# A two-layer attention and graph kernel: the first stretch with ScalarE and VectorE in a written order, and rows' low parts ahead of masks

## The chip, the cores and the metric

The kernel runs on one core of a Trainium2 chip. A core has several engines, each with its own stream of instructions: TensorE (PE in the profile) multiplies matrices and writes only to PSUM, the accumulator memory; VectorE (DVE) and ScalarE (ACT) do elementwise work and read PSUM out; GpSimd (POOL) does small work here and issues loads of weights; SyncE (SP) issues the other transfers between DRAM and SBUF, the core's working memory. ScalarE issues a few transfers too. The metric is the device time of one execution in microseconds (us).

## The reference

x has 64 graphs of 256 nodes with 512 features; adj is one 256 x 256 matrix of zeros and ones that all graphs share. Layer 0 is attention with 8 heads of 64, layer 1 is a product with adj; each adds its input and is normalised.

```python
q, k, v = x @ Wq + bq, x @ Wk + bk, x @ Wv + bv          # heads of 64
scores = einsum('bqhd,bkhd->bhqk', q, k) / sqrt(64)
scores = scores + (1 - adj) * -1e9
out = einsum('bhqk,bkhd->bqhd', softmax(scores), v).reshape(b, n, d)
x = layernorm(x + out @ Wo + bo)
y = einsum('nm,bmd->bnd', adj, x)
x = layernorm(x + y @ W1 + b1)
```

## The kernel before

Work goes by pairs of graphs, p = 0 to 31 (`NP` = 32). All products with weights are made from three parts: a value is split into a high part, a low part and a difference (`high`, `low`, `diff`), and a block of output is 3 x 4 matmuls of 128 x 512 (`product`, L298). A pair takes 4 blocks each with wv ("v"), wq and wk ("q", "k"), wo ("o") and w1 ("l"). Splitting takes ScalarE for the high part (`x_high`, `set_high`) and VectorE for the other two (`rest`, L252). For weights ScalarE works a second time, on the low part (`split`, L121).

**Weights.** Each of five sets of split weights (v, qk1, qk0, o, l) is 3 MB. They are split once, stored in DRAM (`keep`, L129, issued on SP), and loaded again for each pair by `load_w` (issued on POOL) into `wring`, six buffers of 1 MB, three for a set. The stages follow in the order of `STAGES` (L100). wv, wq and wk are split straight in the ring (`split_in_ring`), wo and w1 beside it (`split_aside`, L152), into three of the four buffers named `sh`; wo is read from the `sl` buffers, w1 from `sd`. The same names hold split operands later (`set_high`).

**Attention.** `scores` multiplies k and q and lets ScalarE take the exponential; `masked` multiplies by adj on VectorE and `summed` adds over key chunks (`masks` is two of the first and one of the second); `values` sums the weights for the softmax and multiplies with v. Its `between` list is issued between ScalarE's copy of the sums (`zc`) and of the values (`vc`).

**Layer 1.** The normalised rows are split in two (`hl_high` on ScalarE, `hl_low` on VectorE) into tiles named `hl`, one for each graph b and half of the features. `adj_x(p, b, half)` multiplies such a tile with adj and splits the result out of PSUM (`set_high` on ScalarE, `rest` on VectorE). `hl` comes from the pool `two`, and PSUM tiles of all blocks and of `adj_x` from `ps_mm`:

```python
two = pool("two", 2)
ps_at = pool("ps_at", 5, space=bass.MemoryType.PSUM)
ps_mm = pool("ps_mm", 3, space=bass.MemoryType.PSUM)
```

**Order.** The functions `start`, `first`, `second` and `last` list tasks for `do`, which issues them one by one. Inside `tc.manual_schedule(engines=...)` the named engines execute in the order of the program; instructions of other engines, and of SP's and POOL's queues, are ordered by the framework's planner. `start` and `last` fix TensorE alone; the loop over w = 1 to 31 fixes TensorE, VectorE and ScalarE. In pass w, `first(w)` finishes the attention of pair w − 1 and does blocks v, q and k of pair w and blocks o of w − 1; `second(w)`, w = 1 to 30, does scores of w, the early q and k blocks of w + 1, and layer 1 of w − 1. A tile of a pool whose buffers are all taken waits until the last reader of an earlier tile is done, on whichever engine that reader is; the instruction that first writes the tile does this waiting.

In `start`, the first pair's x is transposed by TensorE in four groups (`x_first`), each copied out of PSUM by ScalarE and VectorE; later pairs are loaded in 64 KB pieces (`load_x`) and transposed by VectorE (`x_t`). `load_r` loads the rows for the residual into tiles named `r`, which at first hold the raw wq and wk.

Of the kernel before, what the change touches and what calls it, by code (L numbers as in the profile page):

```python
# [8 lines left out]
F32 = mybir.dt.float32  # L9
F32R = mybir.dt.float32r  # L10
I32 = mybir.dt.int32
AF = mybir.ActivationFunctionType
# [3 lines left out]
P = 128  # L16
# [19 lines left out]
def fast(tc, x, adj, wq, bq, wk, bk, wv, bv, wo, bo, w1, b1, out):  # L36
# [34 lines left out]
    RAW, SCRATCH, W = {}, {}, {}  # L71
# [10 lines left out]
    def load_r(p):  # L82
        if p < NP:
            t = two.tile([P, 2, NC, D], F32, name="r")
            nc.sync.dma_start(t, xr[p])
            R[p] = [t[:, b] for b in range(2)]
# [34 lines left out]
    def split(raw, parts):  # L121

        high, low, diff = parts
        nc.scalar.activation(high, raw, AF.Copy, scale=CUT)
        nc.vector.scalar_tensor_tensor(low, high.bitcast(F32), -RHO, raw, op0=OP.mult, op1=OP.add)
        nc.vector.scalar_tensor_tensor(diff, high.bitcast(F32), -1 / FINE, low.bitcast(F32), op0=OP.mult, op1=OP.add)
        nc.scalar.activation(low, low.bitcast(F32), AF.Copy, scale=FINE / RHO)
# [8 lines left out]
    def split_in_ring(stage, k):  # L136

        name, p = stage
        if k == 0:
            W[stage] = ring(name)  # L140
        t = [w[:, k // 2, k % 2] for w in W[stage]]
        if name == "v":
            split(RAW["v", k], t)
        else:
            g, which = int(name[2]), "qk"[k // 2]
            raw = RAW[which][:, 2 * (k % 2):2 * (k % 2) + 2, g * HF:(g + 1) * HF]
            split(raw, [u.rearrange("p (k e) -> p k e", k=2) for u in t])
        if k == DC - 1:
            for i in range(3):
                keep(name, i, None, W[stage][i])  # L150

    def split_aside(name, k):  # L152
        t = [four.tile([P, D], F32R, name="sh") for _ in range(3)]
        split(RAW[name, k], t)
        for i in range(3):
            keep(name, i, k, t[i])
# [33 lines left out]
    for k in range(DC):  # L190
        RAW["l", k] = four.tile([P, D], F32, name="sd")
        nc.sync.dma_start(RAW["l", k], w1[k * P:(k + 1) * P])
# [7 lines left out]
    def adj_t():  # L200
# [4 lines left out]
        nc.vector.tensor_copy(adjT, pt)  # L205

# [184 lines left out]
    def masks(p, g, b):  # L391
        return [(masked, p, g, b, 0), (masked, p, g, b, 1), (summed, p, g, b)]
# [74 lines left out]
    def do(*tasks):  # L467
        for t in tasks:
            for f, *args in (t if isinstance(t, list) else [t]):
                f(*args)  # L470
# [9 lines left out]
    def first(w):  # L480
# [4 lines left out]
        do((inverse, q - 1, "l", 1), masks(w, 0, 0),  # L485
# [4 lines left out]
           (block, "v", w, 2), (x_t, n, 0), (block, "v", w, 3), (x_t, n, 1), (stage_end, w),  # L490
           (block, "q", w, 2), (block, "k", w, 2), (block, "q", w, 3), (block, "k", w, 3), (stage_end, w),
# [7 lines left out]
    def second(w):  # L499
# [5 lines left out]
           (adj_x, q, 0, 0), masks(w, 1, 0),  # L505
           (block, "k", n, 0), (hl_high, q, 1, 0), (hl_high, q, 1, 1), (hl_low, q, 1, 0), (hl_low, q, 1, 1),
# [7 lines left out]

    def start():
        do(*((x_first, i) for i in range(4)))
        do((block, "q", 0, 0), (split_in_ring, ("v", 0), 0), (block, "k", 0, 0), (split_in_ring, ("v", 0), 1),
           (x_high, 0, 0), (x_high, 0, 1), (x_rest, 0, 0), (x_rest, 0, 1),
           (block, "q", 0, 1), (split_in_ring, ("v", 0), 2), (block, "k", 0, 1), (split_in_ring, ("v", 0), 3),
           (x_high, 0, 2), (x_high, 0, 3), (x_rest, 0, 2), (x_rest, 0, 3), (adj_t,))  # L520
        scores(0, 0)
        qk = lambda g, p: [(split_in_ring, (f"qk{g}", p), k) for k in range(4)]
        o, l = ([(split_aside, n, k) for k in range(4)] for n in "ol")
        do((block, "v", 0, 0), qk(1, 0)[:2], (block, "v", 0, 1), qk(1, 0)[2:], masks(0, 0, 0),
           (block, "v", 0, 2), (block, "v", 0, 3), (stage_end, 0), masks(0, 0, 1), qk(0, 1)[:2], (x_t, 1, 0), (x_t, 1, 1),
           (block, "q", 0, 2), (block, "k", 0, 2), qk(0, 1)[2:], (block, "q", 0, 3), (block, "k", 0, 3), (stage_end, 0),
           (x_high, 1, 0), (x_high, 1, 1), (x_rest, 1, 0), (x_rest, 1, 1), (x_t, 1, 2), (x_t, 1, 3),
           (x_high, 1, 2), (x_high, 1, 3), (x_rest, 1, 2), (x_rest, 1, 3))
        values(0, 0)
        scores(0, 1)  # L530
        do((bv_wo,), (block, "q", 1, 0), masks(0, 1, 0), o[:2], (block, "k", 1, 0), o[2:], masks(0, 1, 1),
           (block, "q", 1, 1), l[:2], (load_r, 0), (load_r, 1), (block, "k", 1, 1), (stage_end, 0), l[2:],
           (o_high, 0, 0, 0), (o_rest, 0, 0, 0), (o_high, 0, 1, 0), (o_rest, 0, 1, 0))
# [32 lines left out]
    with tc.manual_schedule(engines={PE}):  # L566
        start()
    with tc.manual_schedule(engines={PE, DVE, ACT}):
        for w in range(1, NP):
            first(w)  # L570
            if w < NP - 1:
                second(w)
# [190 lines left out]
```

## Time and profile before

| what | value |
|---|---|
| time, median of three executions | 2526.51 us (2525.65 to 2527.11) |
| profiled execution, its own time | 2527.36 us |
| its span, first to last instruction | 2525.6 us |
| mean granted TensorE clock | 0.992 |
| TensorE busy (matmul) | 2445.6 us, 97% |
| TensorE weight loads | 1937.2 us, 77% |
| VectorE busy | 1685.6 us, 67% |
| ScalarE busy | 1299.9 us, 51% |
| GpSimd busy | 443.7 us, 18% |
| moved by DMA | 609.55 MB, mean 241 GB/s |

A row of the timeline has the start (us from the span's start), the time it lasted, the engine, the line, the operation, what it writes <- what it reads, shapes and a count of like instructions merged in the row; in brackets stands the engine's idle time before it and what ended that. A row of the waits has engine and tile that waited, what ended the waits, and then us in total, number and longest. `SPq` and `ACTq` are instructions that an engine's sequencer issues, transfers above all.

### The profile page before, as it was taken

To read this page: it belongs to the slowest core of one execution; us is meant where nothing else is said; L and a number is where in the kernel's file an instruction comes from. 1 tells how busy PE (TensorE), PEld (TensorE's weight loads), DVE (VectorE), ACT (ScalarE), POOL (GpSimd) and SP (SyncE) were. 2 spreads that over 40 slices of the span, in tenths; PEclk is the share of its full clock that TensorE was granted. 3 is DMA by queue.
4 is the path that set the end of the run, shared out by engine and by line. 5 is a ranking of instruction groups with operands and counts; after the bars stand their busy time and mean duration, and the time that the engine had idled before them with its cause. 6 is when DMAs were issued, how large, how long until landed. Compare 5 with 4: busy or idle time off the path is not lost. (4 is left out here: it accounts for less than half of the span.)

```text
span 2525.6 us, 39920 instructions
## 1 busy us (share of the span) xinstructions
PE 2445.6 (97%) x15886; PEld 1937.2 (77%) x15886; DVE 1685.6 (67%) x2807; ACT 1299.9 (51%) x2418; POOL 443.7 (18%) x726
## 2 busy tenths in 40 slices
PE   7599999999999999999999999999999999999997
PEld 5477787787787777777777777777877877877875
DVE  5566667666768666767666677666676667686665
ACT  5445545545445545455455455455455454455454
POOL 0011211111111111111111111112111111111110
PEclk9899999999999999999999999999999999999998
DMA  7867866877866878767878767779668778668650
GB/s 240 289 221 246 298 230 217 264 242 250 279 224 219 273 243 264 256 227 227 263 241 287 241 224 245 243 249 297 225 218 269 242 250 273 227 220 271 226 201 35
DMA packets 374207, 609.55 MB, mean 241 GB/s; under 512 B 273280, under 2 KB 275584, under 8 KB 313728
## 3 DMA queue, kind: packets, MB, share of 16 engines
q0 software_dynamic: 66528, 484.47, 51.5%
q1 hardware_dynamic: 305376, 120.37, 21.0%
q8 instruction: 127, 2.08, 0.3%
q10 hardware_dynamic: 2112, 2.10, 0.2%
q14 instruction: 64, 0.52, 0.1%
HBM read 557.59 MB, written 49.28 MB: 240 GB/s over the span
## 5 line engine op out<-in xcount | busy, mean ns | idle before, releaser
L311 DVE SCALAR_TENSOR_TENSOR r<-mm,r 128x512 f32<-128x512 f32 x256 | 176.0, 688 | 439.8 <-PE mm L304 437.8
L384 DVE TENSOR_TENSOR e<-e,adjT 128x1024 f32<-128x1024 f32 x256 | 303.9, 1218 | 7.2 <-ACT e L379 6.6
L416 ACT ACTIVATE waste<-r,mean 128x512 bf16<-128x512 f32 x256 | 184.3, 720 | 220.4 <-DVE mean L409 216.3
L304 PE MATMUL mm<-wr,sl 128*128 128x512 f32 x1008 | 274.7, 394 | 3.9 <-DVE sl L254 3.9
L304 PE MATMUL mm<-low,wr 128*128 128x512 f32 x1008 | 275.9, 395 | 0.0
L304 PE MATMUL mm<-high,wr 128*128 128x512 f32 x1008 | 271.0, 390 | 0.0
L304 PE MATMUL mm<-wr,sh 128*128 128x512 f32 x1008 | 270.9, 390 | 0.0
L304 PE MATMUL mm<-wr,sd 128*128 128x512 f32 x1008 | 270.5, 390 | 0.0
L304 PE MATMUL mm<-diff,wr 128*128 128x512 f32 x1008 | 269.7, 389 | 0.0
L379 ACT ACTIVATE e<-at 128x512 f32<-128x512 f32 x512 | 257.7, 627 | 22.8 <-PE at L375 22.8
L422 POOL TENSOR_TENSOR rstd<-squares,power 128x2 f32<-128x2 f32 x128 | 149.2, 1166 | 670.8 <-DVE squares L421 539.7
L433 ACT ACTIVATE r<-r,less,rstd 128x512 f32<-128x512 f32 x256 | 194.2, 806 | 117.9 <-DVE less L427 117.9
L375 PE MATMUL at<-qT,kT 64*128 64x256 f32 x2048 | 251.8, 388 | 0.6 <-ACT e L379 0.5
L375 PEld LDWEIGHTS at<-qT,kT 64*128 64x128 f32 x2048 | 210.7, 186 | 42.1 <-issue 25.7
L345 PE MATMUL at<-e,v 128*32 128x256 f32 x4096 | 232.7, 379 | 0.0
L304 PEld LDWEIGHTS mm<-high,wr 128*128 128x128 f32 x1008 | 189.2, 188 | 41.3
L304 PEld LDWEIGHTS mm<-wr,sh 128*128 128x128 f32 x1008 | 189.8, 188 | 40.1
L304 PEld LDWEIGHTS mm<-wr,sl 128*128 128x128 f32 x1008 | 187.4, 189 | 43.1 <-DVE sl L254 4.9
L304 PEld LDWEIGHTS mm<-wr,sd 128*128 128x128 f32 x1008 | 189.8, 188 | 39.6
L304 PEld LDWEIGHTS mm<-diff,wr 128*128 128x128 f32 x1008 | 189.2, 188 | 40.1
L304 PEld LDWEIGHTS mm<-low,wr 128*128 128x128 f32 x1008 | 181.1, 188 | 42.2 <-issue 10.4
L320 ACT ACTIVATE qT<-mm,bq 128x512 f32<-128x512 f32 x128 | 88.0, 688 | 242.5 <-PE mm L304 242.5
(95 smaller groups left out, 3540.2 us busy)
## 6 DMA issues: line engine op xcount, KB each, us to landing
wr<-qk POOLq DMA_DIRECT2D x183, 1024.0 KB, 8.2
wr<-v POOLq DMA_DIRECT2D x93, 1024.0 KB, 6.8
wr<-o POOLq DMA_DIRECT2D x93, 1024.0 KB, 7.0
wr<-l POOLq DMA_DIRECT2D x93, 1024.0 KB, 8.3
r<-in_x_dram SPq DMA_DIRECT2D x32, 1024.0 KB
x<-in_x_dram SPq DMA_DIRECT2D x496, 64.0 KB
out_dram<-r SPq DMA_DIRECT2D x62, 512.0 KB
qk<-wr SPq DMA_DIRECT2D x6, 1024.0 KB
```

The lines of the kernel that those rows point to most:

```text
L304: nc.tensor.matmul(pm, *pairs[k][i], start=i == 0 and k == 0, stop=i == n - 1 and k == DC - 1)
L311: nc.vector.scalar_tensor_tensor(r, pm, scale, r, op0=OP.mult, op1=OP.add, accum_out=ST[p, name, b][:, c:c + 1])
L320: nc.scalar.activation(T[p, b][:, c].rearrange("p b i -> p (b i)"), pm, AF.Identity, bias=bias[:, j:j + 1], scale=scale)
L345: nc.tensor.matmul(at[h * 32:(h + 1) * 32, a, :], V[p, b][:, kc, col:col + 32], E[p, g, b, kc][:, h % 2, h // 2, :], start=kc == 0, stop=k ...
L375: nc.tensor.matmul(sc[s][:, a, :], K[p, g][r, a, b, kc * P:(kc + 1) * P], Q[p, g][r, a, b, :], start=True, stop=True)
L379: nc.scalar.activation(e[:, s], sc[s], AF.Exp, scale=qscale)
L384: nc.vector.tensor_tensor(e, e, mask[:, kc:kc + 1, :].to_broadcast([P, 4, N]), op=OP.mult)
L416: nc.scalar.activation(waste, R[p][b][:, c], AF.Square, bias=t[0][:, c:c + 1], accum_out=t[1][:, c:c + 1])
L422: nc.gpsimd.tensor_tensor(t[2], t[1], power, op=OP.pow)
L433: nc.scalar.activation(r, r, AF.Identity, scale=t[2][:, c:c + 1], bias=t[3][:, c:c + 1])
```

## The change

It has three parts.

- **`start` in a written order.** ScalarE and VectorE execute `start` as it is listed, like TensorE. For that `split` is cut in `split_high` (one ScalarE operation) and `split_rest` (two on VectorE, one on ScalarE), and `pairs_of` spreads the four pieces of a set of weights over three places in the list: the high parts of two pieces, then rest 0, high 2, rest 1, high 3, then rest 2 and 3. All x_high of the first pair come ahead of the first block, `adj_t` is cut in two (`square_adj` is issued later), x_t(1,2) and x_t(1,3) and their x_high go into the `between` of `values(0, 0)`, and x_rest(1,2) and (1,3) behind `bv_wo`.
- **wo and w1.** wo is split in the second half of `start` and at the beginning of `first(1)`, into twelve tiles that take turns between the names `sh` and `sd`. w1 is read from `hl` buffers in place of `sd`, and split in `first(1)`, behind its v, q and k blocks, into the four quarters of one `r` tile (`SPARE`), which `load_r(1)` takes over afterwards. `load_r(0)` is issued ahead of `values(0, 0)`.
- **`second`.** `hl_high` and `hl_low` of graph b = 1 are issued ahead of `adj_x(q, 0, 0)`, and the masks of (w, 1, 0) behind block k of the next pair. This holds for all 30 passes.

```diff
...
@@ -81,7 +81,7 @@
 
     def load_r(p):
         if p < NP:
-            t = two.tile([P, 2, NC, D], F32, name="r")
+            t = SPARE.pop() if SPARE else two.tile([P, 2, NC, D], F32, name="r")
             nc.sync.dma_start(t, xr[p])
             R[p] = [t[:, b] for b in range(2)]
 
@@ -118,10 +118,12 @@
         if ended[0] + 1 < len(STAGES) and ended[0] > 1:
             load_w(STAGES[ended[0] + 1])
 
-    def split(raw, parts):
+    def split_high(raw, parts):
+        nc.scalar.activation(parts[0], raw, AF.Copy, scale=CUT)
+
+    def split_rest(raw, parts):
 
         high, low, diff = parts
-        nc.scalar.activation(high, raw, AF.Copy, scale=CUT)
         nc.vector.scalar_tensor_tensor(low, high.bitcast(F32), -RHO, raw, op0=OP.mult, op1=OP.add)
         nc.vector.scalar_tensor_tensor(diff, high.bitcast(F32), -1 / FINE, low.bitcast(F32), op0=OP.mult, op1=OP.add)
         nc.scalar.activation(low, low.bitcast(F32), AF.Copy, scale=FINE / RHO)
@@ -133,25 +135,43 @@
         to = SCRATCH[name, i] if k is None else SCRATCH[name, i][:, k // 2, k % 2]
         nc.sync.dma_start(to, part.bitcast(F32))
 
-    def split_in_ring(stage, k):
-
-        name, p = stage
-        if k == 0:
+    def in_ring(f, name, p, k):
+
+        stage = name, p
+        if stage not in W:
             W[stage] = ring(name)
         t = [w[:, k // 2, k % 2] for w in W[stage]]
         if name == "v":
-            split(RAW["v", k], t)
+            f(RAW["v", k], t)
         else:
             g, which = int(name[2]), "qk"[k // 2]
             raw = RAW[which][:, 2 * (k % 2):2 * (k % 2) + 2, g * HF:(g + 1) * HF]
-            split(raw, [u.rearrange("p (k e) -> p k e", k=2) for u in t])
-        if k == DC - 1:
+            f(raw, [u.rearrange("p (k e) -> p k e", k=2) for u in t])
+        if f is split_rest and k == DC - 1:
             for i in range(3):
                 keep(name, i, None, W[stage][i])
 
-    def split_aside(name, k):
-        t = [four.tile([P, D], F32R, name="sh") for _ in range(3)]
-        split(RAW[name, k], t)
+    def ring_high(name, p, k):
+        in_ring(split_high, name, p, k)
+
+    def ring_rest(name, p, k):
+        in_ring(split_rest, name, p, k)
+
+    def aside_high(name, k):
+
+        if name == "o":
+            t = [four.tile([P, D], F32R, name=("sh", "sd")[(3 * k + i) % 2]) for i in range(3)]
+        else:
+            if k == 0:
+                SPARE.append(two.tile([P, 2, NC, D], F32, name="r"))
+            slots = [(3 * k + i) % 4 for i in range(3)]
+            t = [SPARE[0].bitcast(F32R)[:, u // 2, u % 2] for u in slots]
+        ASIDE[name, k] = t
+        split_high(RAW[name, k], t)
+
+    def aside_rest(name, k):
+        t = ASIDE.pop((name, k))
+        split_rest(RAW[name, k], t)
         for i in range(3):
             keep(name, i, k, t[i])
 
@@ -188,7 +208,9 @@
         nc.sync.dma_start(bv_s[:, d:d + 1], bv.rearrange("(g h a i u) -> g a h i u", h=4, a=2, i=32, u=1)[d // 2, d % 2])
     bo_s, b1_s = on_all(bo, "bo"), on_all(b1, "b1")
     for k in range(DC):
-        RAW["l", k] = four.tile([P, D], F32, name="sd")
+        if k % 2 == 0:
+            raw_l = two.tile([P, 2, D], F32, name="hl")
+        RAW["l", k] = raw_l[:, k % 2]
         nc.sync.dma_start(RAW["l", k], w1[k * P:(k + 1) * P])
 
     power = cpool.tile([P, 2], F32, name="power")
@@ -203,6 +225,8 @@
             for c in range(NC):
                 nc.tensor.transpose(pt[:, mc, c * P:(c + 1) * P], adj_s[:, c, mc * P:(mc + 1) * P], ident)
         nc.vector.tensor_copy(adjT, pt)
+
+    def square_adj():
 
         square = two.tile([P, NC, N], F32, name="vc")
         nc.vector.tensor_tensor(square, adj_s, adj_s, op=OP.mult)
@@ -477,18 +501,19 @@
         if 0 <= p < NP:
             end_stage()
 
-    def first(w):
+    def first(w, rest=([], []), more=[[]] * 5):
 
         q, n = w - 1, w + 1
         values(q, 1, [(squared, q - 1, "l", 2), (squared, q - 1, "l", 3)])
         scores(w, 0)
-        do((inverse, q - 1, "l", 1), masks(w, 0, 0),
+        do((inverse, q - 1, "l", 1), masks(w, 0, 0), *rest,
            (o_high, q, 0, 1), (o_high, q, 1, 1), (block, "v", w, 0), (o_rest, q, 0, 1), (o_rest, q, 1, 1),
            (less, q - 1, "l", 1), masks(w, 0, 1),
            (block, "v", w, 1), (normed, q - 1, "l", 2), (normed, q - 1, "l", 3),
            (with_bo, q, 0), (with_bo, q, 1),
-           (block, "v", w, 2), (x_t, n, 0), (block, "v", w, 3), (x_t, n, 1), (stage_end, w),
-           (block, "q", w, 2), (block, "k", w, 2), (block, "q", w, 3), (block, "k", w, 3), (stage_end, w),
+           (block, "v", w, 2), (x_t, n, 0), (block, "v", w, 3), more[0], (x_t, n, 1), (stage_end, w),
+           (block, "q", w, 2), more[1], (block, "k", w, 2), more[2], (block, "q", w, 3), more[3],
+           (block, "k", w, 3), more[4], (stage_end, w),
            (x_high, n, 0), (x_high, n, 1),
            (block, "o", q, 0), (x_rest, n, 0), (x_t, n, 2), (x_high, n, 2),
            (block, "o", q, 1), (mean, q, "o", 0), (squared, q, "o", 0), (squared, q, "o", 1),
@@ -502,8 +527,8 @@
         scores(w, 1)
         do((inverse, q, "o", 1), (with_b1, q, 0),
            (block, "q", n, 0), (less, q, "o", 1), (normed, q, "o", 2), (normed, q, "o", 3),
-           (adj_x, q, 0, 0), masks(w, 1, 0),
-           (block, "k", n, 0), (hl_high, q, 1, 0), (hl_high, q, 1, 1), (hl_low, q, 1, 0), (hl_low, q, 1, 1),
+           (hl_high, q, 1, 0), (hl_high, q, 1, 1), (hl_low, q, 1, 0), (hl_low, q, 1, 1), (adj_x, q, 0, 0),
+           (block, "k", n, 0), masks(w, 1, 0),
            (adj_x, q, 0, 1), masks(w, 1, 1)[:1],
            (block, "q", n, 1), (with_b1, q, 1),
            (adj_x, q, 1, 0), (block, "k", n, 1), (stage_end, n), (adj_x, q, 1, 1), masks(w, 1, 1)[1:],
@@ -512,25 +537,28 @@
            (block, "l", q, 2), (less, q, "l", 0), (normed, q, "l", 0), (normed, q, "l", 1),
            (block, "l", q, 3), (mean, q, "l", 1), (o_high, w, 1, 0), (o_rest, w, 1, 0), (stage_end, q))
 
+    def pairs_of(high, rest, *args):
+
+        h, r = ([(f, *args, k) for k in range(4)] for f in (high, rest))
+        return h[:2], r[:1] + h[2:3] + r[1:2] + h[3:], r[2:]
+
     def start():
-        do(*((x_first, i) for i in range(4)))
-        do((block, "q", 0, 0), (split_in_ring, ("v", 0), 0), (block, "k", 0, 0), (split_in_ring, ("v", 0), 1),
-           (x_high, 0, 0), (x_high, 0, 1), (x_rest, 0, 0), (x_rest, 0, 1),
-           (block, "q", 0, 1), (split_in_ring, ("v", 0), 2), (block, "k", 0, 1), (split_in_ring, ("v", 0), 3),
-           (x_high, 0, 2), (x_high, 0, 3), (x_rest, 0, 2), (x_rest, 0, 3), (adj_t,))
+        do(*((x_first, i) for i in range(4)), *((x_high, 0, i) for i in range(4)))
+        v, qk1, qk0 = (pairs_of(ring_high, ring_rest, *stage) for stage in STAGES[:3])
+        o = pairs_of(aside_high, aside_rest, "o")
+        do((block, "q", 0, 0), (x_rest, 0, 0), (x_rest, 0, 1), v[0], (block, "k", 0, 0), (x_rest, 0, 2), v[1],
+           (block, "q", 0, 1), (x_rest, 0, 3), v[2], (block, "k", 0, 1), (adj_t,))
         scores(0, 0)
-        qk = lambda g, p: [(split_in_ring, (f"qk{g}", p), k) for k in range(4)]
-        o, l = ([(split_aside, n, k) for k in range(4)] for n in "ol")
-        do((block, "v", 0, 0), qk(1, 0)[:2], (block, "v", 0, 1), qk(1, 0)[2:], masks(0, 0, 0),
-           (block, "v", 0, 2), (block, "v", 0, 3), (stage_end, 0), masks(0, 0, 1), qk(0, 1)[:2], (x_t, 1, 0), (x_t, 1, 1),
-           (block, "q", 0, 2), (block, "k", 0, 2), qk(0, 1)[2:], (block, "q", 0, 3), (block, "k", 0, 3), (stage_end, 0),
-           (x_high, 1, 0), (x_high, 1, 1), (x_rest, 1, 0), (x_rest, 1, 1), (x_t, 1, 2), (x_t, 1, 3),
-           (x_high, 1, 2), (x_high, 1, 3), (x_rest, 1, 2), (x_rest, 1, 3))
-        values(0, 0)
+        do(masks(0, 0, 0), (block, "v", 0, 0), qk1[0], (block, "v", 0, 1), qk1[1], (block, "v", 0, 2), qk1[2],
+           (block, "v", 0, 3), (stage_end, 0), masks(0, 0, 1), (square_adj,),
+           (block, "q", 0, 2), qk0[0], (block, "k", 0, 2), qk0[1], (x_t, 1, 0), (x_t, 1, 1),
+           (block, "q", 0, 3), qk0[2], (x_high, 1, 0), (x_high, 1, 1), (block, "k", 0, 3), (stage_end, 0),
+           (x_rest, 1, 0), (x_rest, 1, 1), (load_r, 0))
+        values(0, 0, [(x_t, 1, 2), (x_t, 1, 3), (x_high, 1, 2), (x_high, 1, 3)])
         scores(0, 1)
-        do((bv_wo,), (block, "q", 1, 0), masks(0, 1, 0), o[:2], (block, "k", 1, 0), o[2:], masks(0, 1, 1),
-           (block, "q", 1, 1), l[:2], (load_r, 0), (load_r, 1), (block, "k", 1, 1), (stage_end, 0), l[2:],
-           (o_high, 0, 0, 0), (o_rest, 0, 0, 0), (o_high, 0, 1, 0), (o_rest, 0, 1, 0))
+        do((bv_wo,), (x_rest, 1, 2), (x_rest, 1, 3), (block, "q", 1, 0), masks(0, 1, 0), (block, "k", 1, 0), masks(0, 1, 1),
+           (block, "q", 1, 1), o[0], (block, "k", 1, 1), (stage_end, 0), o[1])
+        return o[2], [(f, 0, b, 0) for b in range(2) for f in (o_high, o_rest)]
 
     def last():
 
@@ -563,10 +591,13 @@
            (normed, p, "l", 2), (normed, p, "l", 3))
 
     PE, DVE, ACT = mybir.EngineType.PE, mybir.EngineType.DVE, mybir.EngineType.Activation
-    with tc.manual_schedule(engines={PE}):
-        start()
     with tc.manual_schedule(engines={PE, DVE, ACT}):
-        for w in range(1, NP):
+        left = start()
+        h, r = ([(f, "l", k) for k in range(DC)] for f in (aside_high, aside_rest))
+        first(1, left, (h[:1], r[:1] + h[1:2], r[1:2] + h[2:3], r[2:3] + h[3:], r[3:]))
+        load_r(1)
+        second(1)
+        for w in range(2, NP):
             first(w)
             if w < NP - 1:
                 second(w)
```

More of the change, by code (lines that the diff above doesn't have):

```diff
@@ L70, in fast @@
     XC, XF, XP, R, Q, K, V, E, SM, O, SET, HL, ST, LN = ({} for _ in range(14))
-    RAW, SCRATCH, W = {}, {}, {}
+    RAW, SCRATCH, W, ASIDE, SPARE = {}, {}, {}, {}, []
     def load_x(p, i):
```

## The prediction

> **What bounds the kernel now.** I read the engines' sums first: TensorE (PE) is busy 2445.6 of 2525.6 us, no other engine over 67%, so time is won or lost only where PE stands still. The list of PE's waits over the whole span says where that is:
>
> ```profile
> engine line waited for: us in total, times, longest us
> PE mm L304 <- ACT v L315: 24.1, 1, 24.1
> PE mm L460 <- DVE hl L450: 20.4, 30, 0.7
> PE mm L233 <- ACT e L237: 8.3, 1, 8.3
> ```
>
> The change aims at these three: one long stop, a small one thirty times (once in each `second`), and one at the start. The timeline of the first 130 us:
>
> ```profile
> 11.77 1.30 ACT L124 ACTIVATE wr<-sh 128x512 fp32r<-128x512 f32 x2 [8.48 <-DMA sh<-in_L_gnn_Wv_dram]
> ...
> 17.42 1.11 PE L233 MATMUL mm<-z,o 128*128 128x128 f32 x4 [8.29 <-ACT e L237]
> 34.83 3.92 PE L375 MATMUL at<-qT,kT 64*128 64x256 f32 x32
> ...
> 38.24 1.89 SPq L134 DMA_DIRECT2D v<-wr  x3
> ...
> 125.93 2.07 PE L304 MATMUL mm<-wr,low 128*128 128x512 f32 x4 [24.09 <-ACT v L315]
> ```
>
> ScalarE (ACT) stands before a split of wv that waits for its transfer, with the copies of x's transposes behind it (8.3 us). Later the splits of wo and w1, through four `sh` buffers of which each split takes three, stand between block v 1,0 and its eviction. PE stops 24.1 us and comes back at half rate: 2.07 us for four matmuls that take 1.07 elsewhere, so 131.21 − 125.93 = 5.28 us for a block of 2.72. The stop costs 24.1 + 2.6 = 26.7 us.
>
> Then one `second` in the regular part, where 76.47 us repeat: PE, ACT and VectorE (DVE) between 243 and 251 us.
>
> ```profile
> 244.47 1.12 PE L460 MATMUL mm<-adjT,hl 128*128 128x256 f32 x8
> 245.42 1.10 PE L304 MATMUL mm<-low,wr 128*128 128x512 f32 x4
> ...
> 248.20 0.28 PE L460 MATMUL mm<-adjT,hl 128*128 128x256 f32 x1
> 249.16 1.10 PE L460 MATMUL mm<-adjT,hl 128*128 128x256 f32 x7 [0.68 <-DVE hl L450]
> 250.09 1.09 PE L304 MATMUL mm<-low,wr 128*128 128x512 f32 x4
> ...
> 244.67 0.69 ACT L320 ACTIVATE kT<-mm,bk 128x512 f32<-128x512 f32 x1 [1.15 <-PE mm L304]
> 245.26 1.14 ACT L445 ACTIVATE hl<-r 128x512 fp32r<-128x512 f32 x2
> 246.30 0.59 ACT L268 ACTIVATE sh<-mm 128x512 fp32r<-128x512 f32 x1
> ...
> 243.55 0.69 DVE L254 SCALAR_TENSOR_TENSOR sl<-sh,mm 128x512 fp32r<-128x512 f32 x1 [5.39 <-ACT sh L268]
> 244.89 2.35 DVE L384 TENSOR_TENSOR e<-e,adjT 128x1024 f32<-128x1024 f32 x2
> 247.27 1.22 DVE L389 TENSOR_TENSOR sm<-e,e 128x1024 f32<-128x1024 f32 x1
> 248.42 1.28 DVE L450 TENSOR_TENSOR hl<-r,hl 128x512 fp32r<-128x512 f32 x2
> ```
>
> `adj_x(1,0)` starts at 248.20 and its second matmul waits for `hl_low`, which stands behind three mask operations. The next block follows 1.89 us later; after the other `adj_x` it is 0.95. So each stop costs 0.94 us, 28 us in all. The point to see is ACT's row at 245.26: two `hl_high` side by side, just after `adj_x(0,1)`.
>
> **The skill.** "TensorE: Matmul & The Clock Gate" (Architectural detail) says that ScalarE and VectorE take work in strict order; the rows above agree, for nothing passes a blocked instruction. The same page (Part 1) has an idle TensorE fall to half clock after a free-running window of about 3.4 us. Here the clock record goes to 0.5 at 103.96 us, 2.1 us after PE stopped, yet the 1.83 us stop at 2483.24 left the following matmuls at full rate: the limit lies near 2 us of idle. "Perfetto Trace Analysis" (Identifying Performance Opportunities) says that a regular bubble can mean too few buffers; the 0.68 us one is order on DVE, but buffers decide below. "DMA: Bandwidth & Descriptors" (Anatomy of one DMA) gives 2.0 us + bytes/436e3, an estimate of 2.6 us for 256 KB; w1's stores here landed 2.3 to 2.7 us after their issue.
>
> **The order in `second` (30 times).** Both `hl_high(1,·)` and both `hl_low` move ahead of `adj_x(0,0)`; the first mask group falls behind block k. But `hl` has two buffers (pool `two`), both holding the tiles of b=0. `hl_high(1,0)` needs `adj_x(0,0)` finished (241.9 us, harmless); `hl_high(1,1)` needs `adj_x(0,1)`, which PE reaches only after block k. Behind it on ACT now stand the high part of `adj_x(0,0)` (L268) and the eviction of block k (L320), and these free two of the three `ps_mm` buffers; the third, freed by q 0's eviction, has gone to `adj_x(0,1)`. So q 1, due on PE at 245.42, has no buffer:
> - `adj_x(0,1)` is read out at 244.47 + 1.15 (start to first reader, as for its sister at 252.84 and 253.99) = 245.62; `hl_high(1,1)` runs 245.62–246.24.
> - ACT starts follow 0.52 apart: L268 at 246.14, k's eviction 246.66–247.35. Waking PE takes 0.06: q 1 at 247.41. By the other buffer: DVE does `hl_low(1,1)` from 246.27, the first low part 246.87–247.55, q 1 at 247.61.
> - So 2.0 to 2.2 us late, some 0.1 for refilling, less the 0.94 that no longer occurs (`hl_low(1,0)` is done by 244.2): **+1.26 us each, 38 us in all** (31 to 41). The later masks are hidden: the last low/diff parts end at 258.0, block l 2 needs them at 260.3; the sums of masks are read in the next `first`.
>
> **The start.** What is removed:
> - x_first: ACT issues its last weight load at 8.00–8.37, then copies; rows landed by 9.02. The fourth group is transposed at 9.2–10.3, block q at about 10.75 instead of 18.96: **−8.2**. Scores start at 26.6 (34.83).
> - The wait of 1.48 before `bv_wo` and the 26.7 of the long stop: **−28.2**. Together −36.4.
>
> What comes back, each from laying the written order out with 0.52 per ACT and 0.61 per DVE operation of 512 columns, 1.15 per mask operation, 2.72 per block:
> - v's copies to DRAM are issued behind all loads on SP (38.24 to 40.13), which this change does not move. Three of 1 MB landed at 45.8, 48.3 and 50.7 in a full DMA (422 to 429 GB/s). The qk0 splits reuse these buffers and compute is now 8 us earlier: its diff part waits till 50.7, ACT's low part behind it, then k 0,3's eviction comes at 58.7 where scores need it at 56.9. `values` between them also has an x_high behind an x_t. Scores end 65.65, not 60.85: **+4.8**.
> - x_rest(1,2) and (1,3) now follow `bv_wo`'s add on DVE; q 1,0 needs their low parts at 69.4 and gets the last at 71.4: **+2.0**, of which before paid 0.45 (q 1,0 took 3.17): +1.5.
> - wo goes over four `sh` and four `sd`; k=3's high waits for k=0's low to land (86.3), ACT is late for `values`: **+0.9**. In `first(1)` o_high(0,1,1) waits for the store of wo's last low part (issued 97.3, landed 99.7), v 1,0 is evicted at 100.9, v 1,3 is due at 99.2: **+1.8**.
> - w1 in the four quarters of an `r` tile: DVE reaches it at 110, four pieces with stores of 2.5 us in between keep DVE till 122.8. Block o 2 waits for k 1,3's eviction (+0.6); DVE and ACT enter the o blocks 5 us late and scores(1,1) wait for `zc` and `vc` (+4.0).
> Sum −36.4 + 4.8 + 1.5 + 0.9 + 1.8 + 4.6 = −22.8; I take **−22** (−30 to −12, since landings are uncertain by 2 us each). The stores and splits themselves are as many as before.
>
> **Sum.** 2525.6 − 22 + 38 = 2541.6 us of span. The profiled execution took 2527.36, 1.8 beside its span, and lies 0.85 above the median; the same difference on the median 2526.51 gives 2542.5, and for some half-rate matmuls I say **2543**.
>
> **Rivals.**
> - *Half clock in every `second`* (0.22): a stop of 2.1 us can fill enough of a window to cut the clock. If it does so in 40% of 30, at 1.7 us (3.41 us of window at half rate), +20: 2562. For: cut after 2.1 us at 103.96. Against: 1.83 us was spared.
> - *Faster* (0.15): block q 1 finds a `ps_mm` buffer in time, the masks were all that made PE wait, and 22 + 28 are won: 2476. What speaks for it is the 20.4 us line; against it, ACT's strict order and two `hl` buffers. It decides at break-even 22/30 = 0.73 us a time: q 1 less than 1.57 us late.
> - *The start wins more and `second` loses less* (0.07): −30 + 31: no change, 2527.
> - *More stops in the start* (0.06): stores wait behind loads and `first(1)` loses half of its gain: −12 + 38, 2553.
> - The forecast itself: 0.50, alone 2533 to 2553.
>
> **How the numbers follow.** Range 2526 to 2568: it leaves out the faster case and the ends of the half-clock one, some 0.2. A difference under 0.2% (5 us) is about what can't be told from none. Slower: 0.49 + 0.22 + 0.06 + 0.01 = 0.78; faster 0.15; same 0.07.
>
> **What would show it.** PE's wait L460 <- `hl` gone; in its place 30 waits of about 2 us of L304 (block q) on ACT `kT` or DVE `sl`; ACT idle about 2 us before the second L445, ended by PE; a regular part of 77.7 us where 76.47 stood. Block q at 10.8 us, q 2,0 of `second(1)` at about 138.5 (161.43). I am wrong if the regular part gets shorter, or if the start wins over 30 us.

## The result, and the profile after

The changed kernel takes **2587.93 us** (2587.04 to 2588.64), the kernel before 2526.81 beside it: a ratio of 1.0243, 95% interval 1.0225 to 1.0260. Slower, as forecast, but 20 us beyond the end of the range (2526 to 2568). The span of the profiled execution is 2585.3 us (2525.6), the mean granted clock 0.980 (0.992).

TensorE's waits of the changed kernel, whole span (in total, times, longest):

```profile
PE mm L328 <- ACT kT L344: 53.5, 30, 1.8
PE mm L328 <- ACT qT L344: 11.4, 1, 11.4
PE mm L328 <- DVE low L278: 6.0, 5, 1.9
...
PE mm L328 <- ACT v L339: 3.5, 1, 3.5
```

The three lines that the change aimed at are gone or small: no wait on `hl`, 0.2 us on `e` at the start, 3.5 us in place of 24.1 before v 1,3. Two have come instead: a wait for the eviction of block k (ScalarE's copy of its result out of PSUM) in every `second`, and one of 11.4 us before block o of the first pair.

**One regular `second`.** The timeline of the changed kernel around the first `adj_x` of pair 1, for the same place as the rows of 243 to 251 us before; product is L328 now, `hl_high` L469, `hl_low` L474, `adj_x` L484, the high part of its result L292, the eviction of q and k L344:

```profile
245.88 1.10 PE L484 MATMUL mm<-adjT,hl 128*128 128x256 f32 x8
248.77 1.19 PE L328 MATMUL mm<-low,wr 128*128 128x512 f32 x4 [1.78 <-ACT kT L344]
...
251.64 1.10 PE L484 MATMUL mm<-adjT,hl 128*128 128x256 f32 x8
...
244.51 0.63 ACT L469 ACTIVATE hl<-r 128x512 fp32r<-128x512 f32 x1
247.02 0.63 ACT L469 ACTIVATE hl<-r 128x512 fp32r<-128x512 f32 x1 [1.88 <-PE mm L484]
247.56 0.58 ACT L292 ACTIVATE sh<-mm 128x512 fp32r<-128x512 f32 x1
248.04 0.68 ACT L344 ACTIVATE kT<-mm,bk 128x512 f32<-128x512 f32 x1
```

Read ScalarE first: the second `hl_high` starts 2.51 us after the first, and TensorE's `adj_x(0,1)` ended that wait. Behind it come L292 and k's eviction, which release PSUM. So q 1 starts at 248.77 where 245.88 + 0.95 = 246.83 was due, 1.94 us late. In exchange `adj_x(1,0)` at 251.64 waits for nothing.

**The start.** The same kernel's timeline, PE, SP's queue, VectorE and ScalarE:

```profile
10.71 15.14 PE L328 MATMUL mm<-e,r 128*128 128x512 f32 x32 [0.48 <-issue]
...
105.57 2.08 PE L328 MATMUL mm<-wr,low 128*128 128x512 f32 x4 [3.47 <-ACT v L339]
...
135.01 2.08 PE L328 MATMUL mm<-wr,sl 128*128 128x512 f32 x4 [11.38 <-ACT qT L344]
...
111.19 0.32 SPq L136 DMA_DIRECT2D l<-r  x1
113.39 9.22 SPq L80 DMA_DIRECT2D x<-in_x_dram  x8
122.71 19.81 SPq L136 DMA_DIRECT2D l<-r  x11
...
132.51 0.69 DVE L128 SCALAR_TENSOR_TENSOR r<-r 128x512 fp32r<-128x512 f32 x1 [10.97 <-DMA l<-r]
...
134.29 0.67 ACT L344 ACTIVATE qT<-mm,bq 128x512 f32<-128x512 f32 x1
```

Block q is 8 us earlier, as forecast. But of w1's twelve stores (`l<-r`) only one leaves SP before eight loads of x for pair 3; these keep SP's queue for 9.2 us. w1's second split reuses the slots (quarters of the `r` tile) of the first. Its low part needs the slot of the one store that left in time, its difference that of a store behind the loads; for the second VectorE waits 11 us, ScalarE waits for VectorE, and q's eviction stands behind that on ScalarE.

**Where the 59.7 us of span are.** I took the starts of `values(w,0)` from both timelines. Before, they are 76.47 us apart throughout the regular part. After, 13 of the 29 distances are 77.62 and 16 are 79.20. In the passes of 79.20 the clock record shows one stretch of 3.41 us at half clock (granted clock 0.5); in the others none. The first of them on TensorE's timeline, with the same stop as above, half clock from 327.11:

```profile
326.39 1.49 PE L328 MATMUL mm<-low,wr 128*128 128x512 f32 x4 [1.78 <-ACT kT L344]
327.68 1.91 PE L328 MATMUL mm<-high,wr 128*128 128x512 f32 x4
```

Four matmuls of this kind take 1.08 us in the pass shown above (at 249.80), and 1.91 here.

| place | forecast | measured |
|---|---|---|
| start, to q 2,0 of `second(1)` (161.43 before, 160.09 after) | −22 | −1.3 |
| 30 waits for the `hl` buffer, 77.62 − 76.47 = 1.15 each | +38 | +34.5 |
| half clock after 17 of them, 79.21 − 77.62 = 1.59 each | 0 (a rival) | +27.0 |
| rest, the end | 0 | −0.5 |
| sum | +16 | +59.7 |

### The profile page after: what moved, and what is told of

The parts are those of the page before. It is cut to its first block, busy times and chain, and to the rows that moved or that the text cites. A ratio compares the mean times of both kernels' runs of the same rounds, so it can differ in the third digit from the quotient of the medians.

```text
span 2585.3 us, 39966 instructions
## 1 busy us (share of the span) xinstructions
PE 2481.8 (96%) x15886; PEld 1962.0 (76%) x15886; DVE 1687.4 (65%) x2807; ACT 1303.6 (50%) x2418; POOL 439.3 (17%) x726
## 4 chain that ended last, share of the span: by engine, by line
PE 91%; ACT 3%; DMA 2%; DVE 2%; SPq 1%; issue 0%; POOL 0%; POOLq 0%; ACTq 0%; DVEq 0%
PE mm L328 67%; PE at L399 9%; PE at L369 8%; PE mm L484 4%; PE at L357 2%; ACT hl L469 1%; ACT kT L344 1%; ACT sh L292 1%; SPq L80 1%; DMA o<-sh 1%; DMA l<-r 1%; DMA qk<-wr 0%; SPq L208 0%; DMA r<-in_L_gnn_Wk_dram 0%; DVE e L408 0%
## 5 line engine op out<-in xcount | busy, mean ns | idle before, releaser
L328 PE MATMUL mm<-low,wr 128*128 128x512 f32 x1008 | 289.8, 410 | 55.2 <-ACT kT L344 53.5
L328 PE MATMUL mm<-wr,sl 128*128 128x512 f32 x1008 | 276.1, 395 | 14.8 <-ACT qT L344 11.4
L328 PE MATMUL mm<-high,wr 128*128 128x512 f32 x1008 | 284.6, 406 | 0.0
L328 PE MATMUL mm<-diff,wr 128*128 128x512 f32 x1008 | 276.5, 397 | 0.0
L328 PE MATMUL mm<-wr,sh 128*128 128x512 f32 x1008 | 271.7, 391 | 0.0
L328 PE MATMUL mm<-wr,sd 128*128 128x512 f32 x1008 | 271.0, 390 | 0.0
L399 PE MATMUL at<-qT,kT 64*128 64x256 f32 x2048 | 258.0, 394 | 8.8 <-ACT vc L372 4.0
L328 PEld LDWEIGHTS mm<-low,wr 128*128 128x128 f32 x1008 | 182.5, 190 | 105.8 <-ACT kT L344 59.6
L399 PEld LDWEIGHTS at<-qT,kT 64*128 64x128 f32 x2048 | 213.5, 189 | 53.5 <-issue 26.1
L344 ACT ACTIVATE qT<-mm,bq 128x512 f32<-128x512 f32 x128 | 88.4, 690 | 298.6 <-PE mm L328 298.6
L328 PEld LDWEIGHTS mm<-high,wr 128*128 128x128 f32 x1008 | 198.7, 197 | 44.7
L474 DVE TENSOR_TENSOR hl<-r,hl 128x512 fp32r<-128x512 f32 x128 | 85.5, 688 | 224.0 <-ACT hl L469 223.9
L328 PEld LDWEIGHTS mm<-wr,sl 128*128 128x128 f32 x1008 | 187.7, 189 | 55.0 <-ACT qT L344 11.8
L328 PEld LDWEIGHTS mm<-diff,wr 128*128 128x128 f32 x1008 | 196.6, 195 | 43.3
L328 PEld LDWEIGHTS mm<-wr,sh 128*128 128x128 f32 x1008 | 190.3, 189 | 40.4
```

The costliest lines, as they stand in the source:

```text
L328: nc.tensor.matmul(pm, *pairs[k][i], start=i == 0 and k == 0, stop=i == n - 1 and k == DC - 1)
L344: nc.scalar.activation(T[p, b][:, c].rearrange("p b i -> p (b i)"), pm, AF.Identity, bias=bias[:, j:j + 1], scale=scale)
L399: nc.tensor.matmul(sc[s][:, a, :], K[p, g][r, a, b, kc * P:(kc + 1) * P], Q[p, g][r, a, b, :], start=True, stop=True)
L474: nc.vector.tensor_tensor(t[:, 1], R[p][b][:, :, half * HF:(half + 1) * HF], t[:, 0].bitcast(F32), op=OP.subtract)
```

## The experiments

**Theory 1.** `second` loses by the two buffers of `hl`, as forecast, and again by the half clock that this stop brings; the start gains little because of w1's splits. **Rivals:** the new order is bad whatever the buffers; the new start spoils the regular part; 79.2 us is something other than the clock; the stop at 135 us comes of a full DMA alone, not of queue and slots.

### Which half of the change: the order in `second`, undone and alone

The changed kernel with the old order in `second`:

```diff
-           (hl_high, q, 1, 0), (hl_high, q, 1, 1), (hl_low, q, 1, 0), (hl_low, q, 1, 1), (adj_x, q, 0, 0),
-           (block, "k", n, 0), masks(w, 1, 0),
+           (adj_x, q, 0, 0), masks(w, 1, 0),
+           (block, "k", n, 0), (hl_high, q, 1, 0), (hl_high, q, 1, 1), (hl_low, q, 1, 0), (hl_low, q, 1, 1),
```

> The changed kernel with the old order of masks and high and low parts in `second`; the start keeps the new order. Theory 1 (the loss of 61 us is all in `second`, and the start gains only 1.3 us because its 11.4 us stop gives back what it won): every regular pass takes 76.5 us again, the 30 waits of product on kT and the half clock of the regular part are gone, and the time is 2523 to 2528 us, no different from the kernel before. Rival (the new start, by where it leaves buffers and queues, is what keeps the passes at 77.6 and 79.2): it stays above 2560 us.

Measured: 2525.9 us, ratio 0.9995 (0.9988 to 1.0002). Passes of 76.43 us (one of 77.36), no wait on `kT`, no half clock between 160 and 2450 us. The kernel before with the new order alone (the same edit the other way round):

> The kernel before with nothing changed but the order of eight tasks in `second`. Theory (the loss is this order with two hl buffers, and the half clock that its 1.78 us stop brings where it falls in one window): waits of product on kT in 30 passes, passes of 77.6 and 79.2 us in a mix, some 61 us above the kernel before: 2580 to 2592 us; with other phases of the windows between 2561 (no half clock at all) and 2610 us (in every pass). Rival (the new start's leftovers take part): less than 2550 us.

Measured: 2587.6 us, 1.0242 (1.0225 to 1.0259): with the old start, the same loss. Its waits (in total, times, longest):

```profile
PE mm L304 <- ACT kT L320: 53.5, 30, 1.8
PE mm L304 <- ACT v L315: 22.8, 1, 22.8
```

The long stop is there and the line of 53.5 us too. All of the loss is in the order of these few tasks; the new start as it stands is worth nothing that can be measured.

### Buffers or order: a third buffer for `hl`

```diff
+    three = pool("three", 3)
...
-            raw_l = two.tile([P, 2, D], F32, name="hl")
+            raw_l = three.tile([P, 2, D], F32, name="hl")
...
-            t = HL[p, b, half] = two.tile([P, 2, NC, HF], F32R, name="hl")
+            t = HL[p, b, half] = three.tile([P, 2, NC, HF], F32R, name="hl")
```

Some small tiles (`rz`, `seen`, `table`, `n_good`) go to one buffer each to make room.

> A third buffer for hl, with the new order kept. Theory 1 (hl_high(1,1) waits for adj_x(0,1) because there are two buffers, and all behind it on ScalarE is late): the 30 waits of product on kT go, with them every half clock of the regular part; passes of 76.5 us or, since the low parts no longer end the wait before adj_x(1,0), down to 75.5 us: 2495 to 2527 us. Rival (the order itself is at fault: masks behind high and low parts, whatever the buffers): the waits move to masks and values, and the passes stay at 77.6 us or more, 2555 us or more.

Measured: 2502.4 us, 0.9902 (0.9886 to 0.9919). No wait on `kT` is left in `second`, none on `hl`, no half clock from 162 to 2475 us; passes of 75.69 us, 0.78 below those of before, most of the 0.94 that a stop before `adj_x(1,0)` had cost. The rival falls: low parts ahead of masks are a gain of 24 us once the early tile has a buffer.

### The same without a buffer: only one half early

```diff
-           (hl_high, q, 1, 0), (hl_high, q, 1, 1), (hl_low, q, 1, 0), (hl_low, q, 1, 1), (adj_x, q, 0, 0),
-           (block, "k", n, 0), masks(w, 1, 0),
+           (hl_high, q, 1, 0), (hl_low, q, 1, 0), (adj_x, q, 0, 0), masks(w, 1, 0),
+           (block, "k", n, 0), (hl_high, q, 1, 1), (hl_low, q, 1, 1),
```

> No third buffer: in `second` only the first half of batch 1 (high and low part) goes ahead of adj_x(0,0) and the masks, and the second half goes behind block k n 0, when adj_x(0,0) has released its buffer. Theory (two buffers are enough if only one part is early; adj_x(1,0) needs the first half early, and no one the second): no waits on kT, none of 0.7 us on hl, passes of 75.6 to 75.8 us as with three buffers, 2499 to 2504 us. Rival (the second half's low part, behind block k and between the masks, is late for adj_x(1,1), or the masks' place matters): a wait on hl or on sm again, passes of 76.4 us or more, 2521 us or more.

The masks go back to their old place here too. Measured: 2498.0 us, 0.9887 (0.9871 to 0.9904), 1 us below the expected range, passes of 75.56 us. Its timeline at the same place, TensorE and ScalarE:

```profile
245.69 1.10 PE L484 MATMUL mm<-adjT,hl 128*128 128x256 f32 x8
246.63 1.20 PE L328 MATMUL mm<-low,wr 128*128 128x512 f32 x4
...
249.48 1.10 PE L484 MATMUL mm<-adjT,hl 128*128 128x256 f32 x8
...
242.19 0.69 ACT L344 ACTIVATE kT<-mm,bk 128x512 f32<-128x512 f32 x1 [0.46 <-PE mm L328]
243.13 0.63 ACT L469 ACTIVATE hl<-r 128x512 fp32r<-128x512 f32 x1 [0.26 <-PE mm L484]
```

The second `hl_high` (243.13) still waits for a matmul of `adj_x`, but k's eviction is ahead of it, and the wait is 0.26 us. q 1 follows `adj_x(0,1)` after 0.94, `adj_x(1,0)` waits for nothing. What hurt was never the early low part of the first half; it was the second half, which nobody needed early. Nor was it the masks: with three buffers they stood in the new place, and nothing waited.

### Is it the clock? Filling the stop, with four matmuls and with one

```diff
+    def keep_warm():
+        pm = ps_at.tile([P, 2, N], F32, name="at")
+        for i in range(4):
+            nc.tensor.matmul(pm.rearrange("p b n -> p (b n)"), adjT[:, 0, 0:P], adjT.rearrange("p c n -> p (c n)"),
+                             start=i == 0, stop=i == 3)
...
-           (adj_x, q, 0, 1), masks(w, 1, 1)[:1],
+           (adj_x, q, 0, 1), masks(w, 1, 1)[:1], (keep_warm,),
```

> Four matmuls whose result isn't used (0.95 us) stand in `second` between adj_x(q,0,1) and block q n 1, where TensorE waits 1.8 us; the wait for the buffer stays. Theory 1 (the wait costs 1.15 us of each pass, and the half clock that follows it in 16 of 29 passes costs 1.59 us more each): the wait as shown falls to some 0.9 us, the half clock goes, all passes take 77.6 us, 2557 to 2566 us. Rival A (79.2 us is not the half clock's doing but another order of arrivals): passes of 79.2 us remain, and the time is 2585 us or more. Rival B (any stop, also one of 0.9 us, brings the half clock): the same 2585 us with half clock still shown.

Measured: 2559.0 us, 1.0130 (1.0114 to 1.0147). All 29 distances are 77.61 us and the regular part has no half clock. Useless work on TensorE makes the changed kernel 29 us faster; the table above puts 27 down to the half clock. Rivals A and B fall.

The traces then gave a rule to test. The starts and ends of half-clock stretches lie on a grid of 3.413 us that runs on through the whole execution. In the five kernels that have this stop and its half clock (the changed one, the order alone, and the three w1 kernels below) I sorted all 152 stops of 1.4 to 1.9 us between 145 and 2450 us by whether they lie in one window of the grid. Of 88 that do, 80 are followed by half clock in the next window, and the 8 others end within 0.1 us of an edge. Of 64 that an edge splits, one is (at 149.55 in the run below that moves x's loads), and the window behind that edge holds another stop of 1.33 us. So 1.78 us in one window, a little over half of it, are just enough. With one filling matmul 1.55 us of stop remain, a little under half:

> As the run with four filling matmuls, but with one (0.24 us, its result isn't used), so that TensorE still stands still for 1.5 us in each pass. Theory (the clock is halved for a window of 3.41 us when TensorE stood still for more than half of the window before: in the changed kernel a stop of which 1.78 us lay in one window always brought it, one of which at most 1.69 us did never): no half clock in the regular part, all passes of 77.6 us, 2556 to 2562 us, as with four. Rival (the chance of a half clock grows with the length of the stop, with no edge): some 40% of the passes still take 79.2 us, 2572 to 2582 us.

Measured: 2560.6 us, 1.0131 (1.0115 to 1.0148). Its waits have this line:

```profile
PE mm L328 <- ACT kT L344: 46.6, 30, 1.6
```

Seven eighths of the stopped time are still there, 17 of the stops lie in one window, and none brings half clock. The limit lies between 1.55 and 1.78 us of one window. The alternation of 77.6 and 79.2 follows: a pass of 77.62 us is 22.74 windows, one of 79.20 is 23.20, so the stop moves on by −0.26 or +0.20 of a window from pass to pass and crosses an edge of the grid back and forth.

### Where the start's gain went: x's loads, slots, and both

Three edits of the changed kernel, with its `second` left as it is. First the x loads: in pass 1, `x_t(2,0)` and `x_t(2,1)`, which free the buffers of eight loads, move behind w1's last split.

```diff
+        both = [(x_t, n, 0), (x_t, n, 1)]
+        early, late = ([], both) if w == 1 else (both, [])
...
-           (block, "v", w, 2), (x_t, n, 0), (block, "v", w, 3), more[0], (x_t, n, 1), (stage_end, w),
+           (block, "v", w, 2), early[:1], (block, "v", w, 3), more[0], early[1:], (stage_end, w),
...
-           (block, "k", w, 3), more[4], (stage_end, w),
+           (block, "k", w, 3), more[4], late, (stage_end, w),
```

> In the pass of pair 1, x_t(2,0) and x_t(2,1) move behind the last split of w1, so that the 16 loads of pair 3's x are issued behind w1's twelve stores on SP's queue. Theory 1 (w1's splits wait 5.6 and 11.0 us for stores that stand behind eight x loads of 9.2 us on that queue, and this is the 11.4 us stop before block o 0): the stop falls below 3 us, q 2,0 of `second`(1) comes 8 to 12 us earlier (148 to 152 in place of 160.1), and the time is 2574 to 2579 us. Rival (the stores are slow because the load of weights takes the DMA engines, and wait with or without the x loads): the stop stays at 8 us or more, and the time within 3 us of the changed kernel's 2588.

Measured: 2583.0 us, 1.0222 (1.0205 to 1.0239). A miss: the stop is 8.4 us. No load stands between w1's stores any more, yet VectorE's rows of this kernel (timeline) still have

```profile
119.64 0.69 DVE L127 SCALAR_TENSOR_TENSOR r<-r,hl 128x512 fp32r<-128x512 f32 x1 [5.93 <-DMA l<-r]
...
132.94 0.69 DVE L128 SCALAR_TENSOR_TENSOR r<-r 128x512 fp32r<-128x512 f32 x1 [9.43 <-DMA l<-r]
```

The rival named a stop of 8 us or more, from stores that are slow beside the loads of weights (6.29 MB by POOL's queue between 100 and 140 us). The other two traces agree. In the kernel before, POOL issued no load of weights while w1 was split (109 to 122 us), since TensorE stood still and freed no buffer of the ring. In the changed kernel three went out from 107.94 to 110.85 and three from 119.40 to 121.75; the store issued at 111.19, ahead of every x load, freed its slot only at 120.85. POOL's row before, and VectorE's after:

```profile
128.30 0.57 POOL L114 DMA_DIRECT2D wr<-o  x1 [39.81 <-PE mm L304]
...
120.85 0.69 DVE L127 SCALAR_TENSOR_TENSOR r<-r,hl 128x512 fp32r<-128x512 f32 x1 [5.59 <-DMA l<-r]
```

In the run with x's loads moved it is the same: the first store leaves at 111.49 and its slot is used at 119.64. So a store takes long with or without the x loads, and twelve parts go through four slots. Second edit: the low part is written over the raw rows, so 8 parts use the slots.

```diff
-            slots = [(3 * k + i) % 4 for i in range(3)]
-            t = [SPARE[0].bitcast(F32R)[:, u // 2, u % 2] for u in slots]
+            high, diff = [SPARE[0].bitcast(F32R)[:, u // 2, u % 2] for u in (2 * k % 4, 2 * k % 4 + 1)]
+            t = [high, RAW[name, k].bitcast(F32R), diff]
```

Both edits together:

> With the x loads of pair 3 behind w1's stores, as in the run before, and the low part of each row block of w1 written over the raw rows, so that 8 parts in place of 12 go through the four slots of r. Theory (the 8.4 us stop that stayed comes from splits that wait for slots, whose stores take 6 to 10 us beside weight loads of 6.3 MB): the stop before block o 0 falls below 3 us, and with it the half clock after it; 2570 to 2577 us. Rival (the DMA engines are the bound in that stretch, whatever the slots, and the high parts wait as long): the stop stays at 6 us or more, 2580 to 2585 us.

Measured: 2569.7 us, 1.0174 (1.0157 to 1.0191). No stop before the o blocks at all, no half clock from 111 to 308 us, q 2,0 at 142.8 us in place of 160.1. Between 100 and 140 us the DMA moved 296 GB/s on the mean, 265 in the run before. It is no emptier, so a full DMA alone does not stop TensorE; it does where a split needs the slot of a store that has not landed. The second edit alone:

> The low part of each row block of w1 in its own raw rows, 8 parts in the four slots, and the x loads of pair 3 left where the change has them, between w1's stores. Theory A (the slots were the cause, the x loads only added to it): the stop before block o 0 stays below 3 us, 2569 to 2575 us as with both edits. Theory B (each of the two delays alone holds the splits up, and both must go): a stop of 5 us or more remains, 2577 to 2584 us.

Measured: 2580.9 us, 1.0214 (1.0197 to 1.0231); the stop is 8.8 us, and VectorE's timeline names its cause:

```profile
134.03 0.69 DVE L128 SCALAR_TENSOR_TENSOR r<-r,hl 128x512 fp32r<-128x512 f32 x1 [11.57 <-DMA l<-r]
```

Eight x loads are again between the stores (114.89 to 122.06 on SP). Theory B holds: each delay alone is nearly as long as both together (8.4 and 8.8 against 11.4), and only with both gone does the stop go. The start then brings 161.43 − 142.78 = 18.65 us.

### Together

Three buffers, both w1 edits, and three moves in the start: `x_high(1,2)` and `(1,3)` behind the `vc` copies; `x_rest(1,2)`, `(1,3)` and the copy of bv (`bv_wide`, taken out of `bv_wo`) ahead of `scores(0,1)`; blocks v 1,0 and 1,1 ahead of wo's last split.

```diff
...
-        values(0, 0, [(x_t, 1, 2), (x_t, 1, 3), (x_high, 1, 2), (x_high, 1, 3)])
-        scores(0, 1)
-        do((bv_wo,), (x_rest, 1, 2), (x_rest, 1, 3), (block, "q", 1, 0),
+        values(0, 0, [(x_t, 1, 2), (x_t, 1, 3)])
+        do((x_high, 1, 2), (x_high, 1, 3), (bv_wide,), (x_rest, 1, 2), (x_rest, 1, 3))
+        scores(0, 1)
+        do((bv_wo,), (block, "q", 1, 0),
...
```

> Three buffers for hl, w1 split with 8 parts in the slots and the x loads behind its stores, and three changes of order in the start: x_high(1,2) and (1,3) behind the copies vc, x_rest(1,2) and (1,3) and the copy of bv ahead of scores(0,1) rather than behind the addition to bo, and blocks v 0 and v 1 of pair 1 ahead of the last split of wo. Expected if all terms come in: from the 2502.4 us of three buffers, -8 to -11 (stop before block o 0 and its half clock), -5 to -7 (waits of 3.0, 0.9, 0.8 us around scores(0,1) and their half clock), -3 (wait of 3.4 us on v): 2480 to 2487 us. If the DMA engines hold the splits of w1 whatever the slots: 2490 to 2497 us.

Measured: 2486.0 us, 0.9837 (0.9820 to 0.9853), in the range, though not by the terms named for it. The waits around `scores(0,1)` fell (3.0 to 2.0 us, the two before q 1,0 gone), but stops of 1.7 and 5.6 us on `kT` before and in the o blocks came. Hence the next, without the blocks v moved, and with one half early in `second` in place of the third buffer:

> One half of batch 1 early in `second` with two buffers (2498.0 us when alone), w1's low parts in its raw rows with the x loads behind its stores (-18.2 us when alone: 2587.9 to 2569.7), and the changes of order around scores(0,1) (values(0,1) at 80.5 us in place of 86.1: -5.6), without the blocks v ahead of the last split of wo, after which stops of 1.7 and 5.6 us had come back. Expected by the sum of these: 2474 us, range 2470 to 2479. If the blocks v had nothing to do with those stops and the earlier q 1,0 brings them: 2480 to 2486 us.

Measured: 2483.9 us, 0.9825 (0.9809 to 0.9841); a miss of the sum by 10 us; it lies in the range of the alternative, but the stops named there did not come. The stops of 1.7 and 5.6 are gone, but that before v 1,3 has grown from 3.5 to 6.1, with half clock from 100.6 to 107.4 us and again from 138.1: TensorE is there at 97.95 in place of 102.10, v's evictions begin only at 103.4 (104.9). Last, wo's low parts in their raw rows too:

```diff
-            t = [four.tile([P, D], F32R, name=("sh", "sd")[(3 * k + i) % 2]) for i in range(3)]
+            high, diff = [four.tile([P, D], F32R, name=n) for n in ("sh", "sd")]
+            t = [high, RAW[name, k].bitcast(F32R), diff]
```

> The run of 2483.9 us, with wo's low parts too written over its raw rows, so that its four high and four diff parts find four buffers each. If the 6.1 us stop before v 3 is wo's last split waiting 4.4 us for stores of earlier parts: the stop falls below 3 us and the half clock of 100.6 to 107.4 us goes at least by half: 2476 to 2481 us. If the buffers sl, now held by the stores of low parts, make o_rest of pair 0 wait instead: within 3 us of 2484, with a wait on sl or v as before.

Measured: **2480.4 us**, 0.9820 (0.9804 to 0.9837), the best of the study, 46.6 us below the kernel before. The time is in the expected range, the reason is not quite: the stop fell to 4.2 us only and its half clock stayed; the second stretch of half clock, from 138 us, is what went. What holds v 1,3 there the trace shows, SP's queue and ScalarE:

```profile
72.35 16.91 SPq L80 DMA_DIRECT2D x<-in_x_dram  x8
...
96.37 0.63 ACT L296 ACTIVATE sh<-o 128x512 fp32r<-128x512 f32 x1 [1.36 <-DMA o<-sh]
```

wo's four high parts are ready from 79 to 83.4 us, but their first store leaves SP at 89.36, behind eight x loads. `o_high` (L296) takes their buffers and waits three times for such a store, 4.0 us in all, ahead of v's evictions. It looks like the queue of w1's stores over again; no run moved these loads.

## Why the prediction was right or wrong

- **"The order in `second`": right, mis-sized little.** `hl_high(1,1)` waited for `adj_x(0,1)`, L292 and k's eviction followed, q 1 came 1.94 us late (2.0 to 2.2 forecast), the wait on `hl` went; 1.15 a pass against 1.26. Every row named under "what would show it" for `second` is there, the pass of 77.6 us in 13 of 29. The third buffer shows the cause, not only the place.
- **"Rivals: half clock in every `second`", set aside at 0.22 and at 0 in the sum: wrong, +27.0 us.** The share and price named there (40% of 30, 1.7 us) were near what came (17 of 30, 1.59). The step that failed is the sentence "1.83 us was spared", from which I made a limit near 2 us. On the grid, that stop began 1.64 us before an edge: 1.64 us lay in one window, 0.19 in the next. It was spared by where it fell, not by its length. Even by that limit a stop forecast at 2.0 to 2.2 us was not safe, and the sum put it at nothing. If stops fall evenly over a window of 3.41 us, one of 2.1 us lies wholly inside one in (3.41 − 2.1) / 3.41 = 38% of cases, close to the rival's 40%; with it the forecast would have been the rival's own 2562. This is an estimate by a rule that only the later runs showed.
- **"The start", term of w1 (+4.6): the second step that failed.** The terms ahead of it held: block q at 10.71 (10.75), `scores(0,0)` at 26.2 (26.6), 3.5 us where 24.1 stood. `scores(0,1)` ended at 68.5 (65.65), after two waits of 2.4 and 3.0 us and a stretch at half clock from 60.9 to 67.7 that I had not charged; v 1,3 came at 105.57 (99.2 + 1.8 = 101.0), 4.6 late. The large piece is w1: q 2,0 came at 160.1 in place of 138.5, 21.6 late, so 17 us came after v 1,3. I had counted w1's stores at 2.5 us each, from a stretch of the trace of before in which neither loads of x nor of weights were under way. I had not asked what `x_t(2,0)` releases, nor which loads a TensorE that no longer stands still sets going: beside them the first store took 9.7 us to free its slot. The two w1 edits gave 17.3 us back (160.1 − 142.8), which is this term.
- The rival "stores wait behind loads" was right for the start, at a chance of 0.06 and 10 us of loss where 20.7 came.
- The sum of these: 2541.6 + 20.7 − 3.5 + 27.0 − 0.5 = 2585.3. By this sum either error alone would have left the time inside the range (2561 without the half clock, 2567 without the start's loss); they fell on the same side.

The Trainium skill ("TensorE: Matmul & The Clock Gate", Part 1) speaks of half clock after at least one idle window of about 3.4 us, on a window that runs freely. The grid of 3.413 us is in these traces as it says; a whole idle window is not needed here: 1.78 us of one are enough, and 1.55 are not. The measurement decides.

## What to carry to other kernels

When a task moves ahead of another on an engine that works in order, ask which buffer it writes, who read that buffer last, and whether that reader stands behind the task's own new followers; move only the part that someone waits for. Judge a short regular stop of TensorE by the part of it that lies in one clock window of 3.41 us, and expect a stop of over half a window to cost half clock in a share of the passes. A buffer that is freed by a store is as late as everything ahead of that store on its queue, so list which loads the tasks around it set free; and take a store's time from a stretch in which the same loads are under way.

## What was not expected of the hardware

- Half clock after 1.78 us of idle TensorE within one 3.413 us window (80 of 88), in one of 64 when an edge split such a stop, and there beside a second one, and never after 1.55 us (17). One such window costs 1.59 us.
- Four matmuls whose result nobody reads made the changed kernel 29 us faster by shortening each stop from 1.78 to 0.85 us; one (to 1.55 us) made it 27 us faster.
- Eight x loads of 64 KB among w1's stores keep SP's queue for 7.2 to 9.2 us, about 1 us each, and a store of 256 KB issued behind them waits all of that.
- A store of 256 KB that leaves ahead of them frees its slot after 9.7 us beside loads of weights (111.19 to 120.85), and after 2.6 us once none is under way (133.89 to 136.53).
